# The planner's TensorE clock moves on to the time at which a product's operands should be done

## The chip, the cores and the metric

One core of one Trainium2 chip runs the whole program. The metric is the device time of one execution in microseconds (us), as the median of several runs. Everything is float32.

## The reference

Eight sequences (B = 8) of 512 tokens with 256 features go through one layer of two halves. The first half is a Mamba block, the second a mixture-of-experts attention with a feed-forward net; the expert attention has 16 heads of 64 features and 8 experts, 2 of them active per token and head.

```python
x = x + layernorm(mamba(layernorm(x)))      # 512 channels, 16 states, a scan over 512 tokens
x = x + layernorm(ffn(layernorm(x)))

def mamba(x):
    x_ssm, z = split(x @ in_proj_w.T)
    xc = silu(causal_conv4(x_ssm) + conv_b)
    dt, Bv, Cv = projections of xc
    h_t = exp(dt_t * A) * h_(t-1) + dt_t * B_t * xc_t        # for 16 states
    y = sum over states (h_t * C_t) + xc * D
    return (y * silu(z)) @ out_proj_w.T

def ffn(src):
    q, k = rope(src Wq), rope(src Wk)                        # per head
    gv, go = gate(src, Wsel_v), gate(src, Wsel_o)            # top 2 of 8 sigmoids
    v = sum over experts gv * (src Wv)
    o = softmax(q k / 8) v
    src = src + sum over heads, experts (o * go) Wo
    src = layernorm(src) * ln1_g + ln1_b
    src = src + relu(src W1 + b1) W2 + b2
    return layernorm(src) * ln2_g + ln2_b
```

## The kernel before

**Who does what.** TensorE (PE) does every product and transpose. VectorE (DVE) does the scans, the gates, the normalizations and most of what is read out of PSUM. ScalarE (ACT) does exponentials and copies out of PSUM, GpSimd (POOL) the sums over experts (lines 932 to 934) and issues some DMAs; SyncE (SP) issues the other DMAs.

**Two kinds of work run beside each other.** The foreground is the attention: for each sequence b, eight pairs of heads, written `(b, pair)`. The background is everything else: the Mamba block of the next sequence (`mamba(b + 1)`, 32 scan steps), the projections of the one after it (`front(b + 2)`), the gates (`heads`) and the feed-forward net of the sequence before (`feed_forward(b - 1)`).

**A pair.** `ahead` puts the pair's products in a fixed list: values `v`, scores `s`, transposed probabilities `t`, and between them the eight output products `add_output(k)` of the pair before; then `attend` multiplies probabilities and values (`ps_o`, line 946). The names of the tiles on the way are: `sin` and `qk` (rotated queries and keys, DVE, then four accumulating DMAs from POOL in `rotate`); `low`, `p`, `total` (softmax); `pt` (transposed probabilities, copied by ACT); `ve` and `v` (values weighted by DVE, summed by POOL); `o`, `gb` and `og` (the attention's output times the gates, DVE, line 978, read by `ps_a`, line 1000).

**A scan step.** Step k of `mamba` takes three DVE instructions on one of four `h` buffers: `h<-bt,dtx` (input), `h<-da,h` (the scan itself) and `h<-h,ct` (times C). POOL then adds the two halves of `h` into `xc` by two accumulating DMAs (`add`, line 574); step k + 4 may use the buffer only when both have landed. These DMAs stand in POOL's one queue together with the sums of `ve`.

**What sets the order of the instructions.** The four compute engines run their instructions in the order in which the Python text emits them (SP's is not among these). That order is made while the program is built, by `_Order`: a planner with a clock for PE (`now`), one for DVE (`vec`), and the time at which the present piece stands (`here`). `pe(us)` moves PE's clock on by the cost of a product. `after` and `then` put a follow-up piece (for example `turned`, `weighted`, `lowest`) into a queue with its due time. The background consists of generators, whose pieces wait in `rest` with a rank. `run()` emits everything that is due up to `now`: follow-ups by their due times, and a background piece whenever DVE's clock leaves room. So how many background pieces stand on DVE between two pieces of a pair depends on how far `now` has gone.

Before a product, `need` makes sure that its operands have been emitted, because an instruction can't wait for one that is not in the text yet:

```python
            def need(self, *what):
                order_of.run(lambda: self.done.issuperset(what))
```

`add_output` does the same for `og` by `order_of.run(lambda: q in self.og)`. If the operands are in the text, the clock is not moved.

Up to a point in `mamba(2)` the planner uses `LEAST_FIRST` (0.1) and no surcharge per DVE instruction; from there on `LEAST` (0.5) and `MORE` (0.09 us) hold (line 693).

Of the kernel before, what the change touches and what calls it, by code (L numbers as in the profile page):

```python
# [97 lines left out]
class _Order:  # L98
# [32 lines left out]
    def _part(self, r, at):  # L131
        self.here, vec = at, self.vec
        wait = next(r[2], None)
        if r in self.rest:
            self.rest.remove(r)
        if wait is None:
            return
        r[0] = max(self.here, self.vec if self.vec > vec else 0.0) + wait
        if isinstance(wait, Free):
            heapq.heappush(self.queue, (r[0], self.n, lambda: self._part(r, r[0])))  # L140
            self.n += 1
        else:
            self.rest.append(r)

    def run(self, until=None):

# [69 lines left out]
def _layers(  # L216
# [4 lines left out]
    with ExitStack() as ctx:  # L221
# [79 lines left out]
        at = dict(step=-1)  # L301
# [495 lines left out]
        class Pair:  # L797
# [3 lines left out]
            def __init__(self, b, pair):  # L801
                self.b, self.pair, self.id = b, pair, f"{b}_{pair}"
                self.xt = inputs_of[b]
                self.p, self.og = {}, {}

                self.final = b == B - 1 and pair == H // 2 - 1

                self.done = set()

            def need(self, *what):  # L810
                order_of.run(lambda: self.done.issuperset(what))

            def project(self):

# [22 lines left out]
            def rotate(self):  # L837

                for j in range(0, P, HP):
                    for to, frm in ((j, j + NROT // 2), (j + NROT // 2, j)):  # L840
                        nc.gpsimd.dma_start(  # L841
                            out=self.qk[to : to + NROT // 2].rearrange("p i s -> p (i s)"),
                            in_=self.sin[frm : frm + NROT // 2].rearrange("p i s -> p (i s)"),
                            accum_op=ALU.add,
                        )
                self.done.add("qk")

            def scores(self, t):


                self.need("qk")
                if t == 0:
                    self.pt = one.tile([P, 2, NT, S], F32, tag="pt", name=f"pt_{self.id}")
                ps = banks(f"ps_s_{self.id}_{t}")
                for j in range(2):
                    feats = slice(j * HP, j * HP + HP)
                    nc.tensor.matmul(  # L857
                        ps[:, j, :], lhsT=self.qk[feats, 0, bass.ts(t, P)], rhs=self.qk[feats, 1, :],
                        start=True, stop=True,
                    )  # L860
                pe(1.13)
                low = small.tile([P, 2], F32, tag="low", name=f"low_{self.id}_{t}")
                p = self.p[t] = work.tile([P, 2, S], F32, tag="p", name=f"p_{self.id}_{t}")
                total = small.tile([P, 2], F32, tag="total", name=f"total_{self.id}_{t}")

                def lowest():
                    vector.tensor_reduce(low, ps, AX.X, ALU.max, negate=True)
                    then(0.0, exponentials)

                def exponentials():  # L870
                    for j in range(2):
                        nc.scalar.activation(  # L872
                            p[:, j, :], ps[:, j, :], AF.Exp, bias=low[:, j : j + 1],
                            accum_out=total[:, j : j + 1],
                        )
                    after(2.0, scaled)

                def scaled():
                    vector.reciprocal(total, total)
                    for j in range(2):  # L880
                        nc.scalar.mul(p[:, j, :], p[:, j, :], total[:, j : j + 1])  # L881
                    self.done.add(("p", t))

                after(0.05, lowest)

            def turn_over(self, t):

                self.need(("p", t))
                pp = banks(f"ps_pt_{self.id}_{t}")
                for j in range(2):  # L890
                    for i in range(NT):
                        nc.tensor.transpose(  # L892
                            pp[:, j, bass.ts(i, P)], self.p[t][:, j, bass.ts(i, P)], ident
                        )
                pe(1.05)

                def copied():
                    nc.scalar.copy(  # L898
                        self.pt[:, :, :, bass.ts(t, P)], pp.rearrange("p j (i q) -> p j i q", q=P)
                    )  # L900
                    self.done.add(("pt", t))

                after(0.05, copied)

# [19 lines left out]
            def weighted(self, k, ps):  # L924
                j, t = k // 2, k % 2 * 2
                ve = work.tile([P, 2, E, HP], F32, tag="ve", name=f"ve_{self.id}_{k}")
                gate = state[self.b][1][:, t : t + 2, 2 * self.pair + j, :]
                vector.tensor_tensor(
                    ve, ps.rearrange("p a (e i) -> p a e i", i=HP),
                    gate.unsqueeze(3).to_broadcast([P, 2, E, HP]), ALU.mult,  # L930
                )
                nc.gpsimd.tensor_tensor(ve[:, :, 0:4], ve[:, :, 0:4], ve[:, :, 4:8], ALU.add)  # L932
                nc.gpsimd.tensor_tensor(ve[:, :, 0:2], ve[:, :, 0:2], ve[:, :, 2:4], ALU.add)  # L933
                nc.gpsimd.tensor_tensor(  # L934
                    self.v[:, j, t : t + 2, :], ve[:, :, 0], ve[:, :, 1], ALU.add
                )
                self.done.add(("v", k))

            def attend(self):

# [22 lines left out]
            def weigh(self, q):  # L963

                spare = self.final and q > 1
                of, tag = (work, "ve") if spare else (wpool, "gb")
                gb = of.tile([P, 2, S], F32, tag=tag, name=f"gb_{self.id}_{q}")
                for j in range(2):
                    r = (2 * self.pair + j) * E + 2 * q
                    nc.sync.dma_start(  # L970
                        out=gb[j * HP : j * HP + HP].rearrange("p e s -> p (e s)"),
                        in_=go_d[self.b][r : r + 2, :].rearrange("e s -> (e s)")
                        .unsqueeze(0).to_broadcast([HP, 2 * S]),
                    )
                og = self.og[q] = work.tile(
                    [P, 2, S], F32, tag="p" if spare else "og", name=f"og_{self.id}_{q}"
                )
                vector.tensor_tensor(og, self.o.to_broadcast([P, 2, S]), gb, ALU.mult)

            def add_output(self, k):  # L980

                if self.pair == 0 and k == 0:
                    sums[self.b] = psum_a.tile([P, ND, S], F32, tag="sum", name=f"ps_a_{self.b}")
                pa, q, i = sums[self.b], k // 2, k % 2
                order_of.run(lambda: q in self.og)
                if i == 0:
                    w = self.wo = wpool.tile(
                        [P, 2, D], F32, tag="wo", name=f"wo_{self.id}_{q}"
                    )
                    for j in range(2):  # L990
                        nc.sync.dma_start(
                            out=w[j * HP : j * HP + HP],
                            in_=wo[2 * self.pair + j][:, q, :].rearrange("(i p) d -> p i d", i=2),
                        )
                if self.b == B - 1:
                    for g in range(2):
                        self.add_half(k, g, self.wo[:, i])
                else:
                    for c in range(ND):
                        nc.tensor.matmul(  # L1000
                            pa[:, c, :], lhsT=self.wo[:, i, bass.ts(c, P)], rhs=self.og[q][:, i, :],
                            start=(self.pair == 0 and k == 0),
                            stop=(self.pair == H // 2 - 1 and k == E - 1),
                        )
                pe(1.71)
                if i == 1 and q + 2 < E // 2:
                    after(0.05, lambda: self.weigh(q + 2))
# [113 lines left out]
        def last_net():  # L1121
# [27 lines left out]

            def outputs(g, ks):  # L1150
                for k in ks:
                    order_of.run(lambda: k // 2 in last.og)
                    last.add_half(k, g, w_o[:, k // 2, k % 2])
                    pe(0.86)
                    order_of.run()
# [117 lines left out]
        last, net = None, last_net()  # L1273
        with tc.manual_schedule(engines=MANUAL):
# [11 lines left out]
            for b in range(B):  # L1286
                for pair in range(H // 2):
# [9 lines left out]
                    last = now  # L1297
# [85 lines left out]
```

## Time and profile before

| | us |
|---|---|
| median of 3 runs | 3668.6 (3666.76 to 3671.24) |
| the profiled execution's own time | 3673.76 |
| its span | 3672.0 |

| engine | busy us | share of the span | instructions |
|---|---|---|---|
| PE | 3406.9 | 93% | 11250 |
| DVE | 3048.9 | 83% | 3198 |
| POOL | 1677.5 | 46% | 1597 |
| ACT | 1664.0 | 45% | 2866 |

The profile is of one execution. Busy is the union of an engine's instructions in the span; idle time stands with each group of instructions, with what ended it. A granted clock below 1 means that TensorE ran part of a stretch at half rate. Since buffer numbers are left out of the names, a pair is found by the copy `o<-ps_o` on ACT (line 952), of which there are 64, one per pair in order: pair (b, p) in this document reaches from its own copy to the next one, so it holds the products that `ahead` puts behind that pair's `attend`.

### The profile page before, as it was taken

Reading aid. Unit: us, or ns where it says so; the run is one execution under the profiler, and the core shown is the slowest. Engines: PE = TensorE matmul, PEld = TensorE weight load, DVE = VectorE, ACT = ScalarE, POOL = GpSimd, SP = SyncE. Lnnn points to the kernel's source line nnn. Section 1 sums busy time; section 2 is a strip of 40 time slices with the busy share of each in tenths; the row PEclk is TensorE's granted clock in tenths of the full one; section 3 lists DMA queues with packets and bytes.
Section 4 is the critical chain, followed back from the end, with each engine's and each line's share of the span. In section 5 each row is a group of like instructions: output and inputs, shape, how many; then the busy total and the mean of one; then the engine's idle time right before and its main releaser. Section 6 shows DMA issues by size and latency. Waiting matters only on the chain.

```text
span 3672.0 us, 35171 instructions
## 1 busy us (share of the span) xinstructions
PE 3406.9 (93%) x11250; PEld 1678.2 (46%) x11250; DVE 3048.9 (83%) x3198; ACT 1664.0 (45%) x2866; POOL 1677.5 (46%) x1597
## 2 busy tenths in 40 slices
PE   5768989989899999999999999999999999999997
PEld 3533334444344444444444444445444444446555
DVE  7878898799989898999989998899988999654443
ACT  5624443545543455344644446444553444332332
POOL 1425663354645545354454555355443657232321
PEclk8879999999999999999999999999999999999999
DMA  4927774577866768577755868568765778443430
GB/s 136 198 73 175 179 173 115 150 181 176 196 144 165 176 169 195 124 182 181 197 139 143 203 154 204 146 154 188 183 171 128 181 186 203 118 126 92 115 106 26
DMA packets 282534, 574.06 MB, mean 156 GB/s; under 512 B 37224, under 2 KB 124520, under 8 KB 282096
## 3 DMA queue, kind: packets, MB, share of 16 engines
q1 hardware_dynamic: 201584, 422.88, 40.0%
q0 software_dynamic: 80768, 148.95, 24.3%
q8 instruction: 91, 1.49, 0.2%
q14 instruction: 91, 0.75, 0.1%
HBM read 403.36 MB, written 19.42 MB: 115 GB/s over the span
## 4 chain that ended last, share of the span: by engine, by line
PE 48%; DVE 27%; issue 8%; DMA 7%; ACT 5%; POOL 5%; SPq 0%; DVEq 0%; POOLq 0%; ACTq 0%
PE ps_v L916 14%; DVE h L175 11%; PE ps_a L1000 9%; DMA xc<-h 5%; PE ps_qk L819 5%; PE ps_s L857 4%; PE ps_a L1020 3%; PE ps_o L946 3%; PE ps_pt L892 3%; DVE ve L175 2%; DVE og L175 2%; DVE low L175 2%; DVE xs L175 2%; PE ps_in L347 1%; DVE hit L175 1%
## 5 line engine op out<-in xcount | busy, mean ns | idle before, releaser
L916 PE MATMUL ps_v<-wv,xt 128*128 128x512 f32 x2048 | 945.8, 605 | 20.4 <-DVE y L175 13.3
L932 POOL TENSOR_TENSOR ve<-ve 128x512 f32<-128x512 f32 x256 | 423.6, 1655 | 1148.1 <-DVE ve L175 996.5
L1000 PE MATMUL ps_a<-og,wo 128*128 128x512 f32 x1792 | 847.1, 606 | 28.0 <-DVE og L175 27.7
L872 ACT ACTIVATE p<-ps_s,low 128x512 f32<-128x512 f32 x512 | 347.3, 683 | 723.0 <-DVE low L175 722.6
L574 POOL DMA_DIRECT2D xc<-h x504 | 463.8, 1099 | 382.1 <-DMA xc<-h 170.0
L916 PEld LDWEIGHTS ps_v<-wv,xt 128*128 128x128 f32 x2048 | 385.9, 193 | 536.9 <-issue 481.3
L175 DVE TENSOR_TENSOR_SCAN h<-da,h 128x1024 f32<-128x1024 f32 x228 | 541.2, 2374 | 10.3 <-ACT da L511 0.4
L1000 PEld LDWEIGHTS ps_a<-og,wo 128*128 128x128 f32 x1792 | 326.5, 192 | 440.9 <-issue 371.4
L881 ACT ACTIVATE p<-p,total 128x512 f32<-128x512 f32 x512 | 341.5, 714 | 252.2 <-DVE total L175 251.4
L175 DVE TENSOR_TENSOR og<-o,gb 128x1024 f32<-128x1024 f32 x256 | 320.1, 1271 | 128.8 <-ACT o L952 81.6
L175 DVE TENSOR_TENSOR ve<-ps_v,gv 128x1024 f32<-128x1024 f32 x256 | 311.7, 1218 | 130.0 <-PE ps_v L916 102.7
L898 ACT COPY pt<-ps_pt 128x1024 f32<-128x1024 f32 x256 | 256.9, 1005 | 347.3 <-PE ps_pt L892 345.9
L511 ACT ACTIVATE da<-dt,decay 128x511 f32<-128x511 f32 x512 | 339.8, 714 | 103.9 <-DVE h L175 100.8
L175 DVE TENSOR_TENSOR h<-bt,dtx 128x1024 f32<-128x1024 f32 x228 | 321.2, 1409 | 34.6 <-DMA xc<-h 34.4
L175 DVE TENSOR_TENSOR h<-h,ct 128x1024 f32<-128x1024 f32 x256 | 338.0, 1320 | 3.8
L175 DVE TENSOR_REDUCE low<-ps_s 128x2 f32<-128x1024 f32 x256 | 310.8, 1214 | 26.8 <-PE ps_s L857 26.1
L933 POOL TENSOR_TENSOR ve<-ve 128x256 f32<-128x256 f32 x256 | 318.1, 1243 | 20.1
L841 POOL DMA_DIRECT2D qk<-sin x256 | 204.5, 1209 | 256.7 <-DVE qk L175 128.9
L857 PE MATMUL ps_s<-qk 64*128 64x512 f32 x1024 | 295.0, 650 | 24.3 <-ACT p L872 14.0
L892 PEld LDWEIGHTS ps_pt<-ident,p 128*128 128x128 f32 x2048 | 239.4, 141 | 124.1 <-issue 87.1
L946 PE MATMUL ps_o<-pt,v 128*64 128x512 f32 x1024 | 249.9, 615 | 30.8 <-POOL v L934 16.7
L892 PE MATMUL ps_pt<-ident,p 128*128 128x128 f32 x2048 | 266.8, 274 | 6.4 <-ACT pt L898 2.6
(165 smaller groups left out, 3579.0 us busy)
## 6 DMA issues: line engine op xcount, KB each, us to landing
gb<-go_d SPq DMA_DIRECT2D x512, 256.0 KB, 4.8
xc<-h POOLq DMA_DIRECT2D x504, 256.0 KB, 5.6
wv<-in_wv_dram SPq DMA_DIRECT2D x128, 512.0 KB, 5.9
wo<-in_wo_dram SPq DMA_DIRECT2D x504, 128.0 KB, 4.0
ct<-bc_d SPq DMA_DIRECT2D x64, 512.0 KB, 5.8
bt<-bc_d SPq DMA_DIRECT2D x57, 512.0 KB, 5.6
wqk<-in_wqk_dram SPq DMA_DIRECT2D x64, 256.0 KB, 2.7
qk<-sin POOLq DMA_DIRECT2D x256, 64.0 KB, 4.8
```

What stands on the lines that cost most here:

```text
L175: return getattr(self.engine, name)(*args, **kw)
L511: nc.scalar.activation(das[k % 2][:, j, 1:S], dt[:, m, 1:S], AF.Exp, scale=decay[:, m, g + j : g + j + 1],)
L574: nc.gpsimd.dma_start(out=xc[:, k % NC, :], in_=hs[k][:, j, :], accum_op=ALU.add)
L857: nc.tensor.matmul(ps[:, j, :], lhsT=self.qk[feats, 0, bass.ts(t, P)], rhs=self.qk[feats, 1, :], start=True, stop=True,)
L872: nc.scalar.activation(p[:, j, :], ps[:, j, :], AF.Exp, bias=low[:, j : j + 1], accum_out=total[:, j : j + 1],)
L881: nc.scalar.mul(p[:, j, :], p[:, j, :], total[:, j : j + 1])
L892: nc.tensor.transpose(pp[:, j, bass.ts(i, P)], self.p[t][:, j, bass.ts(i, P)], ident)
L916: nc.tensor.matmul(ps[:, i, :], lhsT=self.xt[:, c, bass.ts(t + i, P)], rhs=self.wv[:, c, :], start=(c == 0), stop=(c == ND - 1),)
L932: nc.gpsimd.tensor_tensor(ve[:, :, 0:4], ve[:, :, 0:4], ve[:, :, 4:8], ALU.add)
L933: nc.gpsimd.tensor_tensor(ve[:, :, 0:2], ve[:, :, 0:2], ve[:, :, 2:4], ALU.add)
L946: nc.tensor.matmul(po[j * HP : j * HP + HP, 0, :], lhsT=self.v[:, j, t, :], rhs=self.pt[:, j, t, :], start=(t == 0), stop=(t == NT - 1),)
L1000: nc.tensor.matmul(pa[:, c, :], lhsT=self.wo[:, i, bass.ts(c, P)], rhs=self.og[q][:, i, :], start=(self.pair == 0 and k == 0), stop=(self. ...
```

## The change

A product's operands now carry a time. `done` becomes a dictionary from the operand to the planner's time at which it should be finished: the later of `here` and `vec`, plus an allowance for what follows on other engines (4.0 us for the rotation's DMAs, 1.5 for the scaled probabilities, 3.6 for POOL's sums, 0.1 for `og`; 1.2 for the copy of `pt`). `need` first emits what is missing, as before, and then calls `reach` with the latest of these times: if it lies ahead of `now`, PE's clock goes on to it, and everything that has become due in between is emitted ahead of the product. `og` gets an entry too, so `add_output` and `last_net` use `need` as well. The text's instructions stay the same; only their places in the order can differ.

```diff
+    def reach(self, at):
+        if at > self.now:
+            self.now = self.here = at
+            self.run()
...
-                self.done = set()
+                self.done = {}
             def need(self, *what):
-                order_of.run(lambda: self.done.issuperset(what))
+                order_of.run(lambda: all(w in self.done for w in what))
+                order_of.reach(max(self.done[w] for w in what))
+            def ends(self, what, us):
+                self.done[what] = max(order_of.here, order_of.vec) + us
...
-                self.done.add("qk")
+                self.ends("qk", 4.0)
...
-                    self.done.add(("p", t))
+                    self.ends(("p", t), 1.5)
...
-                    self.done.add(("pt", t))
+                    self.done["pt", t] = order_of.here + 1.2
...
-                self.done.add(("v", k))
+                self.ends(("v", k), 3.6)
...
                 vector.tensor_tensor(og, self.o.to_broadcast([P, 2, S]), gb, ALU.mult)
+                self.ends(("og", q), 0.1)
...
-                order_of.run(lambda: q in self.og)
+                self.need(("og", q))
...
-                    order_of.run(lambda: k // 2 in last.og)
+                    last.need(("og", k // 2))
```

## The prediction

> **What bounds the kernel now.** I read the page's busy times first, then its slices, then the same by stage, and only then the waits.
>
> ```profile
> PE 3406.9 (93%) x11250; PEld 1678.2 (46%) x11250; DVE 3048.9 (83%) x3198; ACT 1664.0 (45%) x2866; POOL 1677.5 (46%) x1597
> ...
> PE   5768989989899999999999999999999999999997
> ...
> DVE  7878898799989898999989998899988999654443
> ...
> PEclk8879999999999999999999999999999999999999
> ```
>
> PE is nearly full and its work stays the same, so a new order can win back only idle time: 265 us in all, 97 of them in the first 281 us (before the first pair is done), which the change hardly touches. By sequence (cut at the copy `o<-ps_o`; columns: length, then busy time of PE, PEld, DVE, ACT, POOL, granted clock, DMA):
>
> ```profile
> 281.00:656.00 375.00, 340.30 (x1043) 153.46 (x1042) 331.30 (x317) 159.96 (x287) 203.58 (x179) 0.96 0.68 158
> 656.00:1120.00 464.00, 425.62 (x1324) 197.09 (x1323) 414.24 (x431) 230.91 (x383) 222.26 (x203) 0.97 0.70 169
> 1120.00:1549.00 429.00, 412.71 (x1308) 192.97 (x1308) 387.08 (x403) 208.20 (x352) 219.94 (x200) 0.98 0.72 171
> 1549.00:1974.00 425.00, 410.52 (x1309) 193.08 (x1308) 384.32 (x400) 205.66 (x351) 209.91 (x196) 0.99 0.68 168
> ```
>
> PE idles 35 us in sequence 0 and 38 in sequence 1, against 14 to 16 in each of 2 to 5. So the place to look is 281 to 1120 us. There, one wait is the largest, and DVE's own wait stands behind it (waits of PE and of DVE, 281 to 656 us: total, times, longest):
>
> ```profile
> PE ps_a L1000 <- DVE og L175: 23.6, 5, 6.2
> ...
> DVE h L175 <- DMA xc<-h: 13.8, 4, 4.7
> ```
>
> **The change part by part.** Setting the built programs' orders side by side, pair by pair and engine by engine, shows four things.
>
> (1) *Sequences 2 to 5: the same two orders, exchanged.* The planner falls into a cycle of two orders. Before, sequences 2 and 4 have order X, 3 and 5 order Y; after, 2 and 4 have Y and 3 and 5 X, alike on DVE down to the single instruction (buffer names aside). Both are in the trace: cut at the copy of the pair before, X is 426.5 us (sequence 4) and Y 426.2:
>
> ```profile
> 2022.70:2449.20 426.50, 411.82 (x1308) 192.38 (x1308) 389.11 (x404) 208.60 (x353) 218.43 (x200) 0.98 0.70 171
> 2449.20:2875.40 426.20, 411.19 (x1309) 192.57 (x1310) 384.85 (x402) 205.70 (x350) 211.47 (x197) 0.99 0.68 168
> ```
>
> Exchange costs nothing. But the X of sequence 2 took 428.1 (1168.1 to 1596.3), for one longer wait of `ps_v` for `y` (3.3 us against 1.8): -1.6, if it was due to what came before it. Sequence 6 begins as X before and as Y after; its second pair took 61.7 us in X form, and 58.8 and 59.0 in the Y's: -2.8. Behind that its `ps_out` moves ahead of four products; it waited 2.8 us for `xc` before, and its `xc` moves ahead on DVE too: 0, with 3 either way. Sequence 7 and the tail are instruction for instruction the same: 0. Sum: -4.4.
>
> (2) *Sequence 0, pairs 0 to 4.* PE's order is unchanged. On DVE a pair still has the same 36 instructions, with six scan steps, but shifted: by pair 1 one more step is done. Before, the end of a pair runs `ve`, scan, `h<-h,ct`, `h<-bt,dtx`, scan, `h<-h,ct`, `h<-bt,dtx`, scan, `og`, `og`; after, it runs `ve`, `h<-bt,dtx`, scan, `h<-h,ct`, `h<-bt,dtx`, scan, `h<-h,ct`, `h<-bt,dtx`, scan, `og`, `og`. One `h<-bt,dtx` (1.2 us) moves from ahead of `ve` to behind it. It matters because the last `h<-bt,dtx` needs a DMA that POOL issues behind the three sums of this very `ve`. Pair 2, DVE (start, duration, in brackets the idle time before it):
>
> ```profile
> 374.05 1.23 DVE L175 TENSOR_TENSOR ve<-ps_v,gv 128x1024 f32<-128x1024 f32 x1 [0.47 <-PE ps_v L916]
> ...
> 389.43 1.22 DVE L175 TENSOR_TENSOR h<-bt,dtx 128x1024 f32<-128x1024 f32 x1 [4.42 <-DMA xc<-h]
> 390.76 2.29 DVE L175 TENSOR_TENSOR_SCAN h<-da,h 128x1024 f32<-128x1024 f32 x1
> 392.97 2.33 DVE L175 TENSOR_TENSOR og<-o,gb 128x1024 f32<-128x1024 f32 x2
> ...
> 394.22 6.74 PE L1000 MATMUL ps_a<-og,wo 128*128 128x512 f32 x8 [5.10 <-DVE og L175]
> ```
>
> From `ve` to the landing are 15.4 us; `og` queues behind it, and PE waits 5.1 us and then runs these eight matmuls in 6.74 us instead of 3.70 (granted clock 0.93 in this pair). Pairs 1 to 4 take 47.2, 52.0, 49.6 and 52.0 us, at 46.7 us of DVE work: DVE bounds them, its idle time is the price. Lower bound of the gain: the landing stays where it is after `ve`, and one more 1.2 us of work fills the wait: 1.2 a pair. Upper bound: the trace has the new arrangement once, where pair 3 of sequence 1 ends:
>
> ```profile
> 947.66 1.22 DVE L175 TENSOR_TENSOR ve<-ps_v,gv 128x1024 f32<-128x1024 f32 x1 [0.48 <-PE ps_v L916]
> ...
> 960.43 1.23 DVE L175 TENSOR_TENSOR h<-bt,dtx 128x1024 f32<-128x1024 f32 x1 [0.48 <-DMA xc<-h]
> ...
> 965.23 3.70 PE L1000 MATMUL ps_a<-og,wo 128*128 128x512 f32 x8 [2.50 <-DVE og L175]
> ```
>
> There DVE waits 0.5 us, PE 2.5, at full clock, and the pair that follows, whose DVE order is within an instruction or two that of the new pairs 1 to 4, takes 47.8 us: 50.2 (the mean of the four) less 47.8 is 2.4. Between 1.2 and 2.4 I take 1.9, nearer to the row with the same order: 4 x 1.9 = 7.6, and 1.2 more for the start of pair 5, which waited 3.8 us for `og`. In pair 0 a step moves into an 8.0 us wait of DVE for `gb`; that wait ends with the same DMA, so I give it nothing by itself. Sum: -8.8.
>
> A rule of the Trainium skill speaks against this ("SBUF — State Buffer", section "Who interferes with whom"): a DVE instruction with two SBUF inputs and a GpSimd instruction that reads SBUF exclude each other, and the later one waits for the whole of the first. After, `h<-bt,dtx`, which has two such inputs, follows `ve` directly, just where POOL's first sum starts; by the rule the sums and the DMA behind them slip by up to 1.2 us, and the lower bound becomes 0 a pair (sum for this part: 0 to -1). The trace has this case too: behind the `ve` of 947.66 the sums were done 7.55 us after its start, and behind that of 374.05, where a scan followed, 7.56. The lock is there, but what DVE runs first doesn't change the end. I keep 1.9, and 0 for the range.
>
> (3) *Pairs 5 to 7 of sequence 0.* `ps_out` of sequence 1 (16 matmuls, 7.8 us) moves ahead of `ps_qk`, a half `ps_a` and `ps_v`; its cover is that these are ready anyway, and if `xc` came late, PE would wait up to 2.8 us as sequence 6 does. Taken at 0. In pair 7 ACT's functions alternate more: the built program has 61 activation table loads instead of 57, all four here, at 1.283 us each (the trace's own row): 5.1 us. ACT is busy 35 of 55 us, but DVE's `total` waits for ACT three times in it (1.8, 1.5 and 3.7 us), so it is not all hidden: between 0 and 5.1, I take half, +2.5.
>
> (4) *Sequence 1* is rearranged on all engines. No view gives it one price. Bounds: at best PE waits as little as in 2 to 5 (16 instead of 38): -22. At worst every pair meets the second rival below: +19. What I can see: `ps_out` waited 2.2 and 2.7 us, and `ps_v` behind it 1.6; it moves behind three products (1.05 + 1.13 + 3.70 = 5.9 us), while its `xc` moves back on DVE by four instructions, 3.8 us; that leaves 2. Pair 0 has its four `bn_stats` no more between `og` and `ve`: another 2, an estimate from the 1.46 and 3.94 us that PE waited there for `p` and `pt`. Taken: -4.
>
> Sum: -4.4 - 8.8 + 2.5 - 4 = -14.7 us. Against the profiled execution's own 3673.8 (span 3672.0, and 1.8 around it) that is 3659; its time stands 5.2 above the median of the runs, from which the forecast is 3668.6 - 14.7 = 3654.
>
> **The rivals.** *Hidden anyway.* The lower bounds hold: sequence 0 gains 4 x 1.2 + 1.2 and loses 5.1 on ACT, sequence 1 gains nothing, the rest 1.6: -2.5, about 3666. For it speaks that most DVE pieces only trade places; against it the 47.8 us row. *Sequence 1 reaches the later pace*, and sequence 0 its upper bound (4 x 2.4 + 1.2): -10.8 + 2.5 - 22 - 4.4 = -35, about 3634. For: the same kinds of work. Against: until `mamba(2)` is through, the planner still counts DVE too cheap. *DVE runs ahead in sequence 1 (slower).* The moved clock lets scan steps into the text ahead of softmax pieces: in the new order of pair 3, scan, `h<-h,ct`, `h<-bt,dtx` and scan stand around `ve` ahead of `low`, which had two short ones before. A step is 1.41 + 2.37 + 1.32 = 5.1 us by the page's groups; where a product of 3.7 us was put ahead too, 1.4 stays, else 5.1; 3.2 in the mean over six pairs is +19. Then the sum is -4.4 - 8.8 + 2.5 + 19 = +8, about 3677. It decides once sequence 1 loses over 18 us. Against it: PE's list moves in the same direction (two `ps_x`, a `ps_in` and a `ps_v` now stand ahead of that `ps_s`). *That it does nothing* is excluded by the orders.
>
> **How the numbers follow.** A difference of 0.2%, 7.3 us, is about what a measurement of this kernel can tell. The forecast has 0.45, hidden anyway 0.21, the later pace 0.13, DVE ahead 0.21. Nearly all of the first and third are faster by over 0.2% (0.55), the slow rival gives 0.21, the second and the edges 0.24. The range goes from the later pace (3634) to somewhat beyond the slow one (3682).
>
> **What would show it.** Right: pairs 1 to 4 of sequence 0 at 48 to 49 us, PE's wait for `og` under 15 us there; sequences 2 to 5 at 426 to 427 each; sequence 7 as before. Wrong: the waits for `xc<-h` in sequence 0 unchanged, pair 7 of sequence 0 over 58 us with ACT as the releaser, or more PE waits for `p`, `ve` and `low` in sequence 1 than 38 us.

## The result, and the profile after

The changed kernel takes 3678.4 us (median of 18 runs, 3668.1 to 3687.7) against 3673.35 us for the kernel before (18 runs, 3662.9 to 3682.0). The ratio is 1.0018, 95% interval 1.0010 to 1.0027: slower by 0.18%, about 5 to 7 us. That is less than the 0.2% that the prediction called about what a measurement can tell, but it lies on the other side of the forecast of -14.7 us. A second series of runs gave 1.0009 (0.9998 to 1.0019), so the size of the loss is known only roughly.

The traced execution of the changed kernel took 3672.3 us (span 3670.6), 6 us below the median of its runs, while the trace of before lies at its median. The two spans laid side by side would therefore show a small gain. Only stretches that repeat in several traces are trusted below.

The page after, the lines that answer to those of before:

```profile
PE 3408.8 (93%) x11250; PEld 1680.7 (46%) x11250; DVE 3053.7 (83%) x3198; ACT 1670.0 (45%) x2870; POOL 1669.0 (45%) x1597
...
PE   5768989989898999999999999999999999999997
...
DVE  7878998799989998889989999898989998744443
...
PEclk8879999999999999999999999999999999999999
```

PE's work is the same, and no slice shows the change. By sequence (cut at `o<-ps_o`: sequence 0, sequence 1, sequences 2 to 5; the columns are length, then busy time of PE, PEld, DVE, ACT, POOL, granted clock, DMA share, GB/s), first after, then before:

```profile
279.80:710.20 430.40, 391.32 (x1202) 177.31 (x1202) 367.64 (x355) 197.61 (x337) 215.89 (x195) 0.96 0.67 159
710.20:1171.90 461.70, 422.22 (x1308) 195.69 (x1308) 432.76 (x429) 219.69 (x375) 236.00 (x214) 0.97 0.71 168
1171.90:2874.90 1703.00, 1642.85 (x5232) 768.44 (x5232) 1545.81 (x1609) 828.58 (x1404) 859.77 (x793) 0.99 0.70 170
```

```profile
280.70:711.00 430.30, 392.87 (x1201) 176.68 (x1201) 367.84 (x356) 195.27 (x340) 220.53 (x195) 0.96 0.67 159
711.00:1168.10 457.10, 419.99 (x1309) 195.04 (x1310) 421.56 (x427) 218.05 (x370) 235.32 (x212) 0.97 0.71 169
1168.10:2875.40 1707.30, 1644.99 (x5233) 770.56 (x5234) 1547.00 (x1609) 828.26 (x1404) 859.74 (x792) 0.99 0.70 169
```

Sequence 0 gained nothing. Sequence 1 lost 4.6 us, and length less PE's busy time (its idle time) went from 37.1 to 39.5 us. DVE's busy time there rose by 11 us; two more instructions of 427, a scan and a product with C, make 3.5 us of it, and the rest asks for an explanation of its own. The 4.3 us of sequences 2 to 5 do not repeat: a second trace of the changed kernel has 1708.9 us there.

The wait that the forecast counted on did shrink. Pair 2 of sequence 0 after the change, DVE:

```profile
375.07 1.21 DVE L181 TENSOR_TENSOR ve<-ps_v,gv 128x1024 f32<-128x1024 f32 x1
376.21 1.21 DVE L181 TENSOR_TENSOR h<-bt,dtx 128x1024 f32<-128x1024 f32 x1
377.52 3.62 DVE L181 TENSOR_TENSOR_SCAN h<-da,h 128x1024 f32<-128x1024 f32 x1
...
390.34 1.23 DVE L181 TENSOR_TENSOR h<-bt,dtx 128x1024 f32<-128x1024 f32 x1 [2.54 <-DMA xc<-h]
391.67 2.29 DVE L181 TENSOR_TENSOR_SCAN h<-da,h 128x1024 f32<-128x1024 f32 x1
393.87 2.33 DVE L181 TENSOR_TENSOR og<-o,gb 128x1024 f32<-128x1024 f32 x2
```

and the product on PE behind it:

```profile
395.13 5.17 PE L1011 MATMUL ps_a<-og,wo 128*128 128x512 f32 x7 [5.39 <-DVE og L181]
```

DVE waits 2.5 us in place of 4.4. But the landing comes 15.3 us after `ve` (15.4 before), `og` 18.8 us after it (18.9 before), and PE waits 5.4 us for it (5.1 before).

One more fact comes from the build of the program: `reach` moves the clock three times in all, by 0.7 and 2.8 us in pair (0, 0) and by 1.4 us in the last pair, where no instruction moves. Everywhere else the operands are already due by the planner's own reckoning. All later differences follow from a planner that is 3.5 us further on in its first pair.

### The profile page after: what moved, and what is told of

The parts are those of the page before. It is cut to its first block, busy times and chain, and to the rows that moved or that the text cites. A ratio compares the mean times of both kernels' runs of the same rounds, so it can differ in the third digit from the quotient of the medians.

```text
span 3670.6 us, 35201 instructions
## 1 busy us (share of the span) xinstructions
PE 3408.8 (93%) x11250; PEld 1680.7 (46%) x11250; DVE 3053.7 (83%) x3198; ACT 1670.0 (45%) x2870; POOL 1669.0 (45%) x1597
## 4 chain that ended last, share of the span: by engine, by line
PE 46%; DVE 26%; DMA 8%; issue 8%; POOL 6%; ACT 5%; SPq 0%; DVEq 0%; POOLq 0%; ACTq 0%
PE ps_v L926 14%; DVE h L181 9%; PE ps_a L1011 9%; DMA xc<-h 6%; PE ps_qk L829 4%; PE ps_s L867 4%; PE ps_a L1031 3%; PE ps_o L956 3%; PE ps_pt L902 3%; DVE og L181 2%; DVE ve L181 2%; DVE low L181 2%; DVE xs L181 2%; DVE hit L181 2%; PE ps_in L353 1%
## 5 line engine op out<-in xcount | busy, mean ns | idle before, releaser
L942 POOL TENSOR_TENSOR ve<-ve 128x512 f32<-128x512 f32 x256 | 413.0, 1613 | 1145.3 <-DVE ve L181 1025.4
L956 PE MATMUL ps_o<-pt,v 128*64 128x512 f32 x1024 | 248.5, 611 | 30.1 <-POOL v L944 20.1
```

What stands on the lines that cost most here:

```text
L956: nc.tensor.matmul(po[j * HP : j * HP + HP, 0, :], lhsT=self.v[:, j, t, :], rhs=self.pt[:, j, t, :], start=(t == 0), stop=(t == NT - 1),)
```

## The experiments

**Where the loss lies.** Four kernels ran side by side: the changed kernel again, and three in which the planner's clock is put on at one pair, so that only one part of the new order is left.

```diff
+    def shift(self, us):
+        self.now = self.here = self.now + us
+        self.run()
...
+                    if (b, pair) in {(1, 7): 1.0}:     # in a_17_p3 (1, 7): 3.0, in a_10_p3 (1, 0): 3.0
+                        order_of.shift({(1, 7): 1.0}[b, pair])
                     ahead(now, lambda: follow(b, pair))
```

The changed kernel again, `after_again`, without an edit:

> The changed kernel once more, so that the three others can be laid beside it in the same job. Counted over the whole program, the new `reach` moves the clock three times only: by 0.7 and 2.8 us in the first pair (0, 0), and by 1.4 us in the last pair, where it changes nothing. Everything that differs later follows from a phase 3.5 us further on. From the two traces: about 5 us over the kernel before (0.14%), with seq 0 at 430 us, seq 1 at 462 (457 before), seqs 2 to 5 together at 1703.

Measured: 3676.5 us, ratio 1.0009 (0.9998 to 1.0019); sequence 0 428.3 us, sequence 1 461.2, sequences 2 to 5 1708.9. The loss of sequence 1 repeats (PE idle 39.9 us), the gain of 2 to 5 does not.

The exchange of X and Y alone, `b_17_p1` (before with the shift):

> The kernel before, with the planner's clock put on by 1.0 us at pair (1, 7): the orders of seqs 0 and 1 are instruction for instruction those of before, those of seqs 2 to 6 those of after (X and Y exchanged). Theory A (the loss lies in the new orders of seqs 0 and 1; the exchange costs nothing): 0 to 5 us under the kernel before, seqs 2 to 5 together at 1703 to 1707 us. Theory B (the exchange costs, and the trace of after, one of its quickest, hides it): 5 us over the kernel before, as after. Theory C (the four more table loads in pair 7 of seq 0): as A, since this kernel has 57 loads.

Measured: ratio 0.9995 (0.9986 to 1.0005), sequences 2 to 5 1706.4 us. The exchange costs nothing and gains nothing that can be told.

Sequences 0 and 1 alone, `a_17_p3` (after with the shift). The shift also puts back pairs 6 and 7 of sequence 1, contrary to what the expectation says of it; pairs 0 to 5 are as in after:

> The changed kernel, with the clock put on by another 3.0 us at pair (1, 7): seqs 0 and 1 as in after (61 table loads), seqs 2 to 6 as before. Theory A: 5 to 9 us over the kernel before, seq 1 at 461 to 462 us. Theory B: equal to the kernel before within 2 us. Theory C: 4 to 5 us over before, all of it in pair 7 of seq 0 (59 us against 55) and none in seq 1.

Measured: ratio 1.0010 (0.9999 to 1.0022), 3677.2 us. Sequence 1 456.4 us, with PE idle 36.7: in this trace most of the loss is gone with pairs 6 and 7. The median doesn't confirm it: it is as high as that of the changed kernel beside it.

Sequence 0 alone, `a_10_p3` (after with the shift):

> The changed kernel, with the clock put on by 3.0 us at pair (1, 0): seq 0 as in after up to pair 6 (the new place of `h<-bt,dtx` behind `ve` in pairs 1 to 4), pair 7 nearly as before with 57 table loads, seqs 1 to 7 as before. Theory A in its form 'seq 1 alone': equal to the kernel before within 2 us, pairs 1 to 4 of seq 0 at 201 us as in both traces. If the new place behind `ve` gains what I had forecast (7.6 us in pairs 1 to 4): 193 us there and 7 us under the kernel before. Theory C: equal to before as well, with pair 7 of seq 0 back at 55 us.

Measured: ratio 1.0002 (0.9992 to 1.0012). Pairs 1 to 4 take 201.4 us (200.8 before): the new place of `h<-bt,dtx` gains nothing by itself. Sequence 1, in the old order, has 457.4 us and PE idle 34.7. Pairs 6 and 7 of sequence 0 together take 101.5 us with 57 table loads, and 102.3 to 103.2 in the three kernels above with 61 and the order of after there. A later one with 61, `after_nosum1`, takes 101.5 as well, so the four loads come to between nothing and 2 us.

The converse came later: the old pairs 0 to 4 of sequence 0, and the new sequence 1, `b_06_p35` (before with a shift of 3.5 at pair (0, 6)):

> The kernel before with the planner's clock put on by 3.5 us at pair (0, 6): pairs 0 to 4 of seq 0 keep the order of before, pairs 6 and 7 and seqs 1 to 6 have that of after (61 table loads). Theory A (the loss lies in seq 1): as slow as after, 3 to 6 us over the kernel before, seq 1 at 460 to 462 us with PE idle 39 to 40 us in it (35 in kernels with the order of before), the wait of `ps_o` for `v` in pair 6 at 7.1 us. If the loss came from the new place of the `h<-bt,dtx` in seq 0: equal to before within 2 us.

Measured: 3682.7 us, ratio 1.0027 (1.0016 to 1.0038). Sequence 1:

```profile
716.20:1179.40 463.20, 422.70 (x1308) 195.28 (x1308) 432.64 (x429) 219.82 (x374) 236.25 (x214) 0.97 0.71 168
```

463.2 us, 40.5 of them without PE, as in both traces of after. The other 6 us stand in sequence 0, where pair 5 takes 77.4 us (67.8 before): neither the old nor the new order, but a mixture. Over the seven traces that kept the old order in sequence 1 up to a few single instructions (four of them of kernels further down), PE idles 33.6 to 37.1 us there, mean 35.1; in the three with the new order 39.5, 39.9 and 40.5. That is a difference of 4.9 us, as much as the whole loss. The lengths agree: 453.6 to 460.4 us, mean 456.9, against 461.2 to 463.2. **The place is settled: sequence 1.**

**Why sequence 0 gained nothing.** One more DVE instruction is put into the wait for `xc<-h`, and none is taken away elsewhere.

```diff
+        spare = const.tile([P, 2], F32, name="spare")
...
+                if k == 3 and self.b == 0:
+                    nc.vector.tensor_reduce(spare, angle[:, :, 0, :], AX.X, ALU.max)
                 nc.gpsimd.tensor_tensor(ve[:, :, 0:4], ve[:, :, 0:4], ve[:, :, 4:8], ALU.add)
```

> The kernel before, with one more DVE instruction of about 1.2 us behind the last `ve` of each pair of seq 0 (a maximum over `angle` into a tile that nobody reads; the planner does not count it, so no other instruction moves). It is just what step (2) of the prediction filled the wait for `xc<-h` with. Theory D (a loop sets the period of pairs 1 to 4: `og`, PE's products up to `ps_v`, `ve`, POOL's sums and the DMA behind them, the scan step, `og`): pairs 1 to 4 stay at 201 us within 2, and DVE's waits for `xc<-h` shrink from 13.8 to about 9 us. Theory of the prediction (DVE bounds these pairs): +1.2 a pair, 205.6 us.

Pairs 1 to 4 of that kernel, and pair 2 on DVE:

```profile
334.90:536.00 201.10, 180.88 (x545) 78.28 (x545) 189.88 (x149) 92.27 (x168) 126.55 (x112) 0.97 0.80 182
```

```profile
373.57 1.22 DVE L175 TENSOR_TENSOR ve<-ps_v,gv 128x1024 f32<-128x1024 f32 x1 [0.47 <-PE ps_v L917]
374.71 1.21 DVE L934 TENSOR_REDUCE spare<-angle 128x2 f32<-128x1024 f32 x1
...
388.35 1.22 DVE L175 TENSOR_TENSOR h<-bt,dtx 128x1024 f32<-128x1024 f32 x1 [3.40 <-DMA wo<-in_wo_dram]
```

201.1 us against 200.8 in this one run, with 4.8 us more work put on DVE, and DVE still waits for the landing in each of the four pairs, 9.3 us in all, as expected. (The DMA named is the last event before the step; the wait is the one that was 4.4 us.) So DVE's work as a whole does not bound these pairs. On the way from `og` to the next `ve` it has little slack, though: in before it stands idle there for 0.2 to 1.7 us, and in three of the four pairs `ve` starts 0.1 us after the last `ps_v`. That stretch of the loop belongs to PE and DVE alike.

The run did more than fill the wait, though. `spare` reads one operand from SBUF, and beside it POOL's first sum took 1.27 us, in place of 3.18 in before, where a scan followed `ve`. The last of the three sums, in before, `fill` and after:

```profile
380.29 1.32 POOL L934 TENSOR_TENSOR v<-ve 128x128 f32<-128x128 f32 x1
```

```profile
378.90 1.32 POOL L937 TENSOR_TENSOR v<-ve 128x128 f32<-128x128 f32 x1
```

```profile
381.74 1.32 POOL L944 TENSOR_TENSOR v<-ve 128x128 f32<-128x128 f32 x1
```

It ends 7.56, 6.65 and 7.99 us after the start of `ve`, and the next two pairs repeat this to 0.01 us. So what DVE runs behind `ve` does move the sums, and the 201.1 us of `fill` hold a gain of that kind. That the new order gains nothing doesn't hang on `fill`: pairs 1 to 4 take 199.2 to 201.4 us in the six traces with the new order there, and 199.0 to 201.0 in five with the old.

What the forecast priced did come, in part. From the first `og` of pair 1 to that of pair 5 the old order takes 203.9 to 206.0 us and the new 200.3 to 202.4, in the mean 0.9 us less a pair. But pair 1 pays it back. Its `ve`, and the `og` behind it, before:

```profile
327.70 1.20 DVE L175 TENSOR_TENSOR ve<-ps_v,gv 128x1024 f32<-128x1024 f32 x1
...
339.76 2.33 DVE L175 TENSOR_TENSOR og<-o,gb 128x1024 f32<-128x1024 f32 x2
```

and after:

```profile
326.96 1.21 DVE L181 TENSOR_TENSOR ve<-ps_v,gv 128x1024 f32<-128x1024 f32 x1
...
339.37 1.22 DVE L181 TENSOR_TENSOR h<-bt,dtx 128x1024 f32<-128x1024 f32 x1 [1.46 <-DMA xc<-h]
...
342.90 2.33 DVE L181 TENSOR_TENSOR og<-o,gb 128x1024 f32<-128x1024 f32 x2
```

Being one step ahead, the new order has one scan more between the two, and a wait for the landing that pair 1 did not have: `og` comes 15.9 us after `ve`, not 12.1. These 3.9 us, once, are what the four pairs save.

Then the DMA itself is left out, in `before_noadd`:

```diff
-                if 0 <= k < by_dma:
+                if 0 <= k < by_dma and b != 1:
```

> The kernel before without the accumulating DMAs `xc<-h` of `mamba(1)`: the sum over the states of sequence 1 is left out. No instruction moves on PE, DVE or ACT. If the landing of that DMA is the part of the loop that costs (theory D): DVE no longer waits for `xc<-h`, PE's waits for `og` in pairs 1 to 4 fall from about 5 us to under 2, and the pairs take 46 to 47.5 us, 184 to 190 in all against 201. If the pairs are held by something else, they stay at 201.

One run: 3666.5 us, where the median of before was 3671.3; pairs 1 to 4 194.9 us. PE's waits in them, before and without the DMA (total, times, longest):

```profile
PE ps_a L1000 <- DVE og L175: 13.5, 3, 5.4
```

```profile
...
PE ps_pt L892 <- ACT pt L898: 4.6, 3, 1.5
PE ps_a L1000 <- DVE og L175: 1.8, 3, 0.6
```

The waits for `og` go, so the landing was what held `og` back. But of the 11.7 us only 5.9 are gained: `pt` is late next. The pairs end at 48.7 us, not at the 46 to 47.5 I had expected.

The last two try to profit from the loop: `og` ahead of the step that waits.

```diff
-                    after(0.8 + 0.1 * q, lambda q=q: self.weigh_soon(q))
+                    after((-4.0 if early(self) else 0.8) + 0.1 * q, lambda q=q: self.weigh_soon(q))
...
+                if q == 1 and early(self):
+                    order_of.least = LEAST_FIRST
...
+                if part == 't3' and early(n):       # in og_7: part == 7; early: b == 0, pairs 1 to 5
+                    order_of.least = 8.0
```

> The kernel before, with the first two `og` of pairs 1 to 5 of seq 0 put ahead of the scan step that waits for `xc<-h`: from the product t3 on the planner holds the background back (`least` at 8 us) until they are in the text, and they are due 4 us before the end of `ps_o`. Seqs 1 to 7 keep the order of before; the scan steps held back end up in pairs 5 to 7 of seq 0. Theory D: `og` leaves the loop, PE's waits for it in pairs 1 to 4 fall from about 5 us to under 1, the pairs take 45 to 47.5 us (before 47 to 52); of the 12 to 15 us saved, the held-back steps cost up to 6 again in pairs 5 to 7. The program: 5 to 13 us under the kernel before. Theory of the prediction (DVE bounds the pairs): little gain, 0 to 2 us, since DVE's work stays the same and only its order changes.

> The same with the background held back only from the last `add_output(7)` on, so that more steps stay within the pairs. Theory D: as og_t3, 5 to 13 us under the kernel before, with a little less left for pairs 5 to 7; a pair that keeps three scan pieces behind `ve` may still wait 1 to 2 us for `xc<-h`, but behind `og`, at no cost to PE. Theory of the prediction: 0 to 2 us.

Measured: ratios 1.0044 (1.0032 to 1.0057) and 1.0045 (1.0031 to 1.0059), so slower. Pairs 1 to 4 took 198.3 us in both, 2.5 less than before. In `og_t3`, DVE's wait in pairs 1 to 4 and PE's in pair 6:

```profile
DVE og L175 <- ACT o L952: 24.1, 4, 7.0
```

```profile
PE ps_x L335 <- DVE qk L175: 10.9, 1, 10.9
PE ps_x L335 <- ACT xs L404: 5.4, 1, 5.4
```

`og` now stood too early: at the head of DVE's order, which is strict, it waited 24 us for `o`, scan steps were pushed into pair 6, and this pair took 87.1 us in place of 50.0. The expectation of 5 to 13 us was wrong, because it priced the wait of PE and not the wait that the move makes on DVE.

**Why sequence 1 lost.** The first suspicion was DVE's 11 us. In the new order, instructions with two inputs from SBUF stand where POOL sums. In pair 4 of after, DVE and POOL:

```profile
1000.21 1.22 DVE L181 TENSOR_TENSOR h<-h,ct 128x1024 f32<-128x1024 f32 x1
1001.35 2.30 DVE L181 TENSOR_TENSOR h<-bt,dtx 128x1024 f32<-128x1024 f32 x1
```

```profile
1000.38 2.18 POOL L942 TENSOR_TENSOR ve<-ve 128x512 f32<-128x512 f32 x1 [0.25 <-DVE ve L181]
```

`h<-bt,dtx` issues at 1001.35 beside a sum that ends at 1002.56, and takes 2.30 us in place of 1.22: it stands still until the sum is over. In pairs 0 to 5 of sequence 1, `h<-bt,dtx`, `z`, `x` and `w<-u` take about 12 us more than their free durations in the three traces with the new order, and 1.2 to 1.4 in those with the old. But this counts only what loses more. `h<-h,ct` and others lose less in the new order, and DVE's whole busy time in these pairs is 330.6 to 331.2 us, against 325.0 to 326.5 in the seven traces with the old: about 5 us more. The other 7 of the 11 us stand in pairs 6 and 7, which have five more instructions. The 12 us of the count, over twice the whole difference, were put into the old order, with the `spare` instruction above in sequence 1:

```diff
+                if self.b == 1 and k < {1: 1, 2: 3, 3: 1, 4: 1, 5: 2, 6: 2}.get(self.pair, 0):
+                    nc.vector.tensor_reduce(spare, angle[:, :, 0, :], AX.X, ALU.max)
```

> The kernel before with ten more DVE instructions of 1.21 us (a maximum over `angle`, one input from SBUF, result unused, unknown to the planner) behind `ve` in seq 1: 1, 3, 1, 1, 2 and 2 for pairs 1 to 6. That is what the traces of after show DVE losing there: `h<-bt,dtx`, `z`, `x` and `w` behind a `ve` take 11.9 us longer in pairs 0 to 5 while POOL sums. Theory E (this lost DVE time is the cause of the loss in seq 1): 3 to 6 us over the kernel before, all in seq 1, and the wait of `ps_o` for `v` in pair 6 goes from 4.3 to about 7 us. Rival F (DVE has slack there, PE's waits came from where the products stand): under 1.5 us, the wait stays at 4.3.

Measured: 3678.9 us, ratio 1.0015 (1.0006 to 1.0024). So DVE time in sequence 1 has a price: 12.1 us of instructions cost about 5.5. (DVE's busy time rose by 7.1 only, to 428.7 us: what stands behind them collides less, by an estimate from the durations 4 us less.) But PE's waits are not those of after:

```profile
PE ps_out L685 <- DVE xc L175: 7.3, 1, 7.3
PE ps_o L949 <- POOL v L937: 4.3, 1, 4.3
```

```profile
PE ps_o L956 <- POOL v L944: 7.4, 2, 7.1
...
PE ps_out L690 <- DVE xc L181: 2.9, 1, 2.9
```

The first two lines are of `fill1`, the last two of after. The lost time of `fill1` came out at `ps_out`; that of after stands at the `ps_o` that ends pair 6, which `fill1` left at 4.3 us as before.

So the collisions were taken away from both orders, by leaving out two of POOL's three sums in sequence 1:

```diff
+                if self.b != 1:
                     nc.gpsimd.tensor_tensor(ve[:, :, 0:4], ve[:, :, 0:4], ve[:, :, 4:8], ALU.add)
                     nc.gpsimd.tensor_tensor(ve[:, :, 0:2], ve[:, :, 0:2], ve[:, :, 2:4], ALU.add)
```

> The kernel before without the first two of POOL's three sums of each `ve` in seq 1 (its values are then not summed over all experts); no other instruction moves. `v` is ready about 3 to 4 us earlier after each `ve`, so the wait of `ps_o` for `v` in pair 6 (4.3 us) falls to about 1. `h<-bt,dtx`, `z`, `x` and `w` lose under 2 us to POOL in pairs 0 to 5, as in before. Seq 1 at 450 to 455 us under both theories; it is the base for the other run.

> The changed kernel with the same two sums left out in seq 1. The time that DVE loses in pairs 0 to 5 falls from 12 to under 4 us. Theory E (the collisions with the sums are the cause): seq 1 within 1.5 us of before_nosum1, where the kernels with all sums differ by 4 to 5. Rival F (the places of the pieces are the cause, the collisions only go along): seq 1 still 4 us longer than in before_nosum1.

Measured: ratios 0.9939 (0.9924 to 0.9954) and 0.9954 (0.9937 to 0.9970), 3649.3 and 3655.8 us. Sequence 1 of the two, and its wait of `ps_o`:

```profile
709.50:1144.10 434.60, 411.91 (x1309) 192.37 (x1310) 402.13 (x427) 217.69 (x370) 150.98 (x156) 0.99 0.74 177
```

```profile
PE ps_o L947 <- POOL v L935: 1.3, 1, 1.3
```

```profile
709.60:1150.50 440.90, 412.60 (x1308) 192.09 (x1308) 410.03 (x429) 219.38 (x375) 144.15 (x158) 0.99 0.74 176
```

```profile
PE ps_o L957 <- POOL v L945: 4.0, 1, 4.0
```

The collisions are nearly gone in pairs 0 to 5 (1.6 us in the second kernel, none in the first), yet the new order is still 6.3 us longer, with PE idle 28.3 us against 22.7, and the medians differ by as much (6.4). Theory E falls: the places of the pieces make a loss of this size without the collisions. Whether the collisions add to it where all sums are run was not separated.

The wait of `ps_o` keeps its difference of 2.7 to 2.8 us in every comparison, and `a_17_p3`, which has it at 4.3, points to its cause, for up to pair 6 its sequence 1 is that of after. PE at the start of pair 6 (cut off at 1077 us), and the wait at its end, after:

```profile
1068.36 3.60 PE L926 MATMUL ps_v<-wv,xt 128*128 128x512 f32 x8
1071.88 1.13 PE L867 MATMUL ps_s<-qk 64*128 64x512 f32 x4
1072.94 3.70 PE L1011 MATMUL ps_a<-og,wo 128*128 128x512 f32 x8
1076.48 0.81 PE L726 MATMUL ps_sel<-w_sel,xt 128*128 128x256 f32 x3
...
1121.21 1.12 PE L956 MATMUL ps_o<-pt,v 128*64 128x512 f32 x2 [7.09 <-POOL v L944]
```

and in `a_17_p3`:

```profile
1066.18 3.60 PE L931 MATMUL ps_v<-wv,xt 128*128 128x512 f32 x8
1069.62 3.62 PE L731 MATMUL ps_sel<-w_sel,xt 128*128 128x256 f32 x16
1073.17 1.13 PE L872 MATMUL ps_s<-qk 64*128 64x512 f32 x4
...
1116.27 1.12 PE L961 MATMUL ps_o<-pt,v 128*64 128x512 f32 x2 [4.32 <-POOL v L949]
```

In the new order the gates' product `ps_sel` stands behind `ps_s` and `ps_a`: it starts 9.7 us after the pair's start, not 5.0. The gates' chain on DVE hangs on it (its first piece, `a<-s`, at 30.1 us in place of 24.5), DVE works without a pause from there to the pair's last `ve` (at 49.4 in place of 46.6), and POOL's `v` and `ps_o` follow that. A delay of 4.7 us at the head of the chain came out as 2.8 at its end. The order of PE's groups in the two pairs differs by this one alone, and it is over half of the 4.9 us: pair 6 takes 58.1 us in all three traces with the new order, 55.2 in `a_17_p3`, and 53.6 to 54.6 in the seven with the old. Still, the chain is read from traces: DVE's order differs too, and no run moved `ps_sel` alone. The rest of the loss was not taken apart; pairs 0 to 5 take 356.2 to 356.7 us against 352.0 to 357.4, which can't be told apart.

**A version better than both** was sought by telling the planner what a `ve` costs DVE beside POOL.

```diff
+                order_of.vector(2.3)      # in after_lock1_1: 1.1, if self.b == 1
                 nc.gpsimd.tensor_tensor(ve[:, :, 0:4], ve[:, :, 0:4], ve[:, :, 4:8], ALU.add)
```

> The kernel before, in which the planner's DVE clock is put on by 2.3 us behind each `ve`, so that it sets fewer background instructions behind it: `low`, which reads PSUM, follows `ve` directly 21 times of 32 in seqs 2 to 5 (14 to 16 before), `h` or `z` 6 times (5 to 9). A try at a version better than both. Theory E: DVE loses less time to POOL's sums, 0 to 10 us under the kernel before; against it speaks that the background then lags, and the waits for `xc` or `sz` at the end of a sequence can grow by as much: 5 us over it.

> The changed kernel, in which the planner's DVE clock is put on by 1.1 us behind each `ve` of seq 1 only: `low` follows `ve` directly 20 times there (15 in after), `h` 4 times (6); seq 0 to pair 6 and seqs 2 to 6 stay as in after. Theory E: `h<-bt,dtx`, `z`, `x` and `w` lose 4 to 8 us less to POOL in seq 1, and 2 to 5 us of the loss come back (program 0 to 2 us over the kernel before). Rival F: the waits of seq 1 change by chance, within 4 us either way.

Measured: ratios 1.1109 (1.1090 to 1.1127) and 1.0041 (1.0028 to 1.0054). In the second, pairs 0 to 5 of sequence 1 take 327 us in place of 357, with collisions down to 5.3 us, and pair 6 then 100.7 in place of 58.1. Both rows of that kernel:

```profile
704.00:1031.20 327.20, 311.40 (x977) 143.38 (x977) 297.81 (x289) 169.28 (x283) 173.86 (x158) 0.99 0.74 177
1031.20:1131.90 100.70, 63.22 (x195) 32.57 (x193) 89.88 (x110) 32.51 (x55) 34.60 (x32) 0.82 0.51 118
```

The first kernel pays the same in every sequence (pair 6 takes 130.7 us in sequences 2 to 5, where `ps_out` waits 32.4 us for `xc`). Background that DVE holds back is not saved: its chain from the last scan step over `ps_out`, the norms, `ps_sel` and the gates to `ve` then stands bare at the sequence's end. Of the kernels that leave nothing out, none beats the one before by more than its interval.

## Why the prediction was wrong, by its own steps

- **Step (2), sequence 0, -8.8: wrong by all of it.** The sentence "DVE bounds them, its idle time is the price" failed: with 1.2 us more put into the wait of each pair, DVE still waited 1.1 to 3.4 us for the landing, and the four pairs took 201.1 us. And the step that moves in pair 0, of which it says "I give it nothing by itself", had a price: it puts one more scan and a wait for the landing ahead of the `og` of pair 1, 3.9 us. The lower bound, 1.2 us a pair, was nearly right (0.9 measured), and these 3.9 us cancel it. PE's wait for `og` in sequence 0 rose from 23.6 to 29.4 us, where under 15 was to be the sign of being right. The analogous row, 47.8 us, was a pair of sequence 1 and did not carry over. My other doubt there, the Trainium skill's rule of "SBUF — State Buffer", section "Who interferes with whom", came true on DVE: beside POOL's sums a scan took 3.62 us and `h<-bt,dtx` 2.30 in place of 2.29 and 1.22. I had asked only when the sums end, and that reading was wrong too: "what DVE runs first doesn't change the end" held for two rows (7.55 and 7.56 us), but the new order has 7.99 and `fill` 6.65.
- **Step (4), sequence 1, -4: the wrong sign, measured +4.6 in the trace and +5.2 between the means of the ten traces above.** Its two named terms came true: the `ps_out` waits fell from 2.2 and 2.7 to 2.9 us in all (2.0 predicted), and PE's idle time in pair 0 from 6.5 to 5.0. What it left out decided: `ps_sel`, moved behind two products, had no price, and the pair that holds it took 58.1 us in place of 54.6.
- **Step (1), -4.4: none of it.** The exchange is free (`b_17_p1`), but the -1.6 and -2.8 were the scatter of one trace (the pair of 61.7 us takes 58.6 to 61.9 in other traces with the same order). Sequences 2 to 5 took 1707.3 and 1706.4 us in the traces of before and of the exchange alone, and 1703.0 and 1708.9 in two of the changed kernel.
- **Step (3), +2.5: too high.** Pair 7 took 59.2 us in place of 55.1, which is what I had named as a sign of the loads, but pair 6 took 44.0 in place of 50.0: the work had only moved between the two. Pairs 5 to 7 together took 172.5 us, and 172.9 before.
- **The rivals.** "Hidden anyway" was right on sequence 0 as a whole. "DVE runs ahead in sequence 1" has the right side and place and wrong working: it needed 18 us there against gains that did not come; about 5 were enough. Its sign, over 38 us of PE waits for `p`, `ve` and `low` there, did not come: they fell from 14 to 13 us while PE's idle time rose. That the clock hardly moves was a rival that I had not thought of: the change acts three times. So the sign of the result is in good part luck, and says little of the idea behind the change: it came from a shift of 3.5 us, and bare shifts of the same clock gave 0.9995 (`b_17_p1`) and 1.0027 (`b_06_p35`).

## What to carry to other kernels

An idle time on the busiest engine is a gain only if its work sets the time at which the wait begins. Fill the wait with a useless instruction first, and look whether the wait is still there and whether the instruction moved anything else: if the stage keeps its time, it is a loop of latencies, and only its links count. Look at the first turn of such a loop by itself, for a new order can pay there what it saves in each turn. When a planner's order is disturbed, price every product that moves back by the chain that hangs on it, not only the waits that get better; and look at how often an edit acts before reasoning on what it says.

## What the runs showed of the hardware

- A GpSimd sum and a VectorE instruction with two SBUF inputs exclude each other for the whole of the earlier one (1.22 to 2.30 us for `h<-bt,dtx`, 2.29 to 3.62 for a scan), also in the scan, while a maximum over one SBUF input keeps its 1.21 us behind a `ve`. What VectorE runs behind `ve` moves the end of the three sums: it came 6.65 us after the start of `ve` with that maximum first, 7.56 with a scan first, and 7.99 in the new order, where `h<-bt,dtx` and a scan follow.
- The sums cost more than POOL's busy time tells: without two of three in one sequence of eight, the program is 22 us shorter, although POOL is busy only 51% of that sequence. Two things went with them, the latency from `ve` to `v` and 19.5 us of VectorE's busy time there (421.6 to 402.1); which of them counts was not separated. A shorter way from `ve` to `v` is the lead that these runs leave; it was not tried.
- PE's granted clock goes with the idle time: 0.99 in sequence 1 without those sums, 0.97 with them, 0.82 in the bare pair of `after_lock1_1`. In the trace of before it is 0.50 from 394.3 to 400.2 us, just behind a wait of 5.1 us, and the eight matmuls there took 6.74 us in place of 3.70.
